# Layer 3's rows of the last image from x and z, with the product of two layers' weights, in a four-layer convolution and attention kernel

## The chip, the core and the metric

The kernel runs on one core of a Trainium2 chip. The metric is the device time of one execution in microseconds (us); lower is better. Before the change three executions took 2698.12 to 2698.23 us, median 2698.2.

## The reference, cut to what matters

Two images of 512 channels and 32 x 32 pixels go through four layers. Layers 0 and 1 (attention with offsets and a multilayer perceptron; attention by channel products with a batch normalization) aren't touched. Layer 2 is attention over the 1024 pixels with 128 middle channels; layer 3 is attention with one channel each for theta, phi and g, plus a squeeze-and-excitation weight.

```python
# layer 2
scores = jnp.einsum('bcn,bcm->bnm', f_x, g_x) * scale
attn = jax.nn.softmax(scores, axis=-1)
z = jnp.einsum('bnm,bcm->bcn', attn, h_x).reshape(B, mid, H, W)
z = conv1x1(z, wv, bv)
return z + x
# layer 3
x_avg = jnp.mean(x, axis=(2, 3), keepdims=True)
se_mid = jax.nn.relu(conv1x1(x_avg, se1_w, se1_b))
W_cw = jax.nn.sigmoid(conv1x1(se_mid, se2_w, se2_b))
g_x = conv1x1(x, g_w, g_b).reshape(b, N)
theta_x = conv1x1(x, theta_w, theta_b).reshape(b, N)
phi_x = conv1x1(x, phi_w, phi_b).reshape(b, N)
f_div_C = jax.nn.softmax(theta_x[:, :, None] * phi_x[:, None, :], axis=-1)
y = jnp.einsum('bij,bj->bi', f_div_C, g_x)
return W_cw * bn(conv1x1(y, W_w, W_b)) + x
```

Layer 3's rows theta, phi and g are linear in layer 2's output, which is x + wv z + bv. So w3 (x + wv z + bv) = w3 x + (w3 wv) z + w3 bv, and the rows can be had from layer 2's input x and from z, without layer 2's output.

## The kernel before, in words

Everything is float32, with channels on the 128 partitions, in four blocks of 128, and pixels along the free dimension, 1024 per image. Layers 0 and 1 take the first 2550 us or so. The last part of the program runs layers 2 and 3 for image 0, with layer 2 of image 1 woven in, and ends with the function `last` for image 1. `last` is written out by hand: each of its instructions goes through `pin`, which keeps it in program order on its engine. The rest is ordered by a scheduler. Each engine executes its own queue in order; semaphores stand where one engine needs another's result or a buffer that another still reads.

Image 0 ends in `l3_out`: `py`, the mean spread over all partitions, lies in two PSUM banks; VectorE reads it once (L1656), ScalarE scales the first result (L1657) and reads `py` three times (L1659), VectorE adds x to these three (L1660), and four stores go out on SP (L1661).

`last` then does this, in halves of 512 pixels:

- `out_z` (L1693): z, eight accumulating matmuls for each half, then a ScalarE copy to SBUF (L1694);
- `out_x` (L1699, L1702): for each half and block of channels one matmul of z with `l2wv`, and on VectorE the sum of that, the bias and x, written over x, with its pixel sum in `xavg`;
- `row` (L1711, L1716): the rows of layer 3, four matmuls for each half, one for each block of channels, each into 32 partitions of its own of `prow`, with weights `w3x`; then a ScalarE copy to `rows3` that adds the biases `b3` (L1672, L1674);
- `spread` (L1723) puts phi and g on all partitions (`pscore`), `turn` (L1728) transposes theta to the partitions (`ptl`), `theta` (L1732) adds up the four blocks' parts, `extremes` (L1735, L1736) finds the largest and smallest phi, and L1810 to L1812 make the exponents' offset of it;
- `exponential` (L1741, ScalarE, eight times) and `weighted` (L1754, VectorE, eight times): the softmax' numerator, denominator and weighted sum, with three buffers `e3` between them;
- the squeeze-and-excitation: `avg` (L1816, L1817), four matmuls (L1821), `mid` on ScalarE (L1826), four matmuls (L1828), `cw` and `aff` (L1831 to L1840);
- `raised` (L1776, GpSimd): the constant part added to x; `mean` (L1759, L1760, L1764): the weighted mean y, spread over all partitions (`pyl`);
- `final` (L1780, VectorE) or `final_act` (L1785 on ScalarE, then L1786 on GpSimd): the output, and its store (L1768, SP).

PSUM has eight banks. Four hold the two `pscore` tiles; two are a pool `ps` with two buffers, for `pz`, `pr2` and `pyl`; the last two are image 0's pool `gps` with one buffer of two banks (`py` is its last tile), and after it, in `last`, a pool `gpl` of two buffers of one bank each, for `prow`, `ptl` and `psel`:

```python
with tc.tile_pool(name="gps", bufs=1, space=PSUM) as gps:
    nd, part = l3_scores(0, gp, gps)
    ...
    l3_out(0, gp, gps, nd)
with tc.tile_pool(name="gpl", bufs=2, space=PSUM) as gps:
    last(1, fp, gp, fps, ps, gps, at2, ht)
```

Of the kernel before, what the change touches and what calls it, by code (L numbers as in the profile page):

```python
# [16 lines left out]
P = 128  # L17
# [3 lines left out]
KC = C // P  # L21
# [51 lines left out]
def conv_seq(  # L73
# [61 lines left out]
    with ExitStack() as ctx_l0:  # L135
# [51 lines left out]
        def pin(ins):  # L187
            return tc.keep_in_program_order(ins) if started else ins
# [890 lines left out]
    xsum = late.tile([P, KC, NT // 512], F32, name="xsum")  # L1079
    l2w = late.tile([P, KC, 3, MID], F32, name="l2w")  # L1080
    nc.sync.dma_start(l2w, l2_w)
    l2wv = late.tile([P, C], F32, name="l2wv")
    nc.sync.dma_start(l2wv, l2_wv)
    se1w = late.tile([P, KC, SE], F32, name="se1w")
    nc.sync.dma_start(se1w, se1_w)
# [576 lines left out]

    def last(b, fp, gp, fps, ps, gps, at2, ht):

        pin = tc.keep_in_program_order
        ve, pe, act = nc.vector, nc.tensor, nc.scalar

        b3 = gp.tile([P, 1], F32, name="b3")
        for i, name in enumerate(("theta", "phi", "g")):
# [4 lines left out]
                else ve.scalar_tensor_tensor(b3, ident[:, i : i + 1], v(f"L3_conv_{name}_b"), b3, ALU.mult, ALU.add)  # L1674
            )
        z = fp.tile([P, HW], F32, name="z")
        rows3 = gp.tile([P, 2, 512], F32, name="rows3")
        th = gp.tile([P, 8], F32, name="th")
        ext = gp.tile([P, 2, 2], F32, name="ext")
# [6 lines left out]
        def at(o, half):  # L1686
            return x[:, o, b * HW + half * 512 : b * HW + (half + 1) * 512]

        def out_z(half):
            pz = ps.tile([P, 512], F32, name="pz", tag="ps")  # L1690
            for t in range(8):
                rhs = at2[:, t, half * 512 : (half + 1) * 512]
                pin(pe.matmul(pz, lhsT=ht[:, t, :], rhs=rhs, start=(t == 0), stop=(t == 7)))  # L1693
            pin(act.copy(z[:, half * 512 : (half + 1) * 512], pz))  # L1694
# [9 lines left out]
                )  # L1704
            )

        def row(half, k):
            if k == 0:
                prow[half] = gps.tile([P, 512], F32, name=f"prow{half}", tag="l3")
            pin(  # L1710
                pe.matmul(  # L1711
                    prow[half][k * 32 : (k + 1) * 32, :], lhsT=w3x[:, k, :], rhs=at(k, half), start=True, stop=True
                )
            )
            if k == KC - 1:
                pin(act.activation(rows3[:, half, :], prow[half], AF.Identity, bias=b3))  # L1716


        pp = [fps.tile([P, 2, 512], F32, name="pscore") for _ in range(2)]
# [1 line left out]
        def spread(half, i):  # L1721
            to_all = c("sel3")[:, i : i + 1].to_broadcast([P, P])
            pin(pe.matmul(pp[i][:, half, :], lhsT=to_all, rhs=rows3[:, half, :], start=True, stop=True))  # L1723
# [63 lines left out]
            store(o, half, r)  # L1787

        es, py = {}, {}
        out_z(0)  # L1790
        out_z(1)
        for o in range(KC):
            out_x(0, o)
        for o in range(KC):
            out_x(1, o)
        for half in range(2):
            for k in range(KC):
                row(half, k)
        spread(0, 0)
        turn(0)  # L1800
        spread(1, 0)
        turn(1)
        extremes(0)
        theta(0)
        spread(0, 1)
        spread(1, 1)
        extremes(1)
        theta(1)
# [2 lines left out]
        pin(ve.tensor_scalar(nm[:, 1, :], th, top[:, 0:1], -1.0, ALU.mult, ALU.mult))  # L1811
        pin(ve.scalar_tensor_tensor(nm[:, 0, :], th, top[:, 1:2], nm[:, 1, :], ALU.mult, ALU.min))  # L1812
        exponential(0)

        avg = gp.tile([P, KC], F32, name="avg")
        pin(ve.tensor_tensor(avg, xavg[:, :, b, 0], xavg[:, :, b, 1], ALU.add))  # L1816
# [2 lines left out]
        for k in range(KC):  # L1819
            pin(  # L1820
                pe.matmul(  # L1821
                    pse[0:SE, 0, 0:1], lhsT=se1w[:, k, :], rhs=avg[:, k : k + 1], start=(k == 0), stop=(k == KC - 1)
                )
            )
        mid = gp.tile([SE, 1], F32, name="mid")
        pin(act.activation(mid, pse[0:SE, 0, 0:1], AF.Relu, bias=v("L3_conv_se1_b")[0:SE]))  # L1826
        for o in range(KC):
            pin(pe.matmul(pse[:, 1, o : o + 1], lhsT=se2w[:, o * P : (o + 1) * P], rhs=mid, start=True, stop=True))  # L1828
        weighted(0)
        cw = gp.tile([P, KC], F32, name="cw")  # L1830
        pin(ve.tensor_tensor(cw, pse[:, 1, 0:KC], v("L3_conv_se2_b"), ALU.add))  # L1831
        exponential(1)
        exponential(2)
        pin(act.activation(cw, cw, AF.Exp, scale=-1.0))
        weighted(1)
        weighted(2)
        pin(ve.tensor_scalar(cw, cw, 1.0, None, ALU.add))
        pin(ve.reciprocal(cw, cw))
        aff = gp.tile([P, 2, KC], F32, name="aff")
        pin(ve.tensor_tensor(aff, l3s, cw.unsqueeze(1).to_broadcast([P, 2, KC]), ALU.mult))  # L1840
        for half in range(2):
            for o in range(3 + half):
                raised(o, half)
        exponential(3)
        weighted(3)
        mean(0)
        for t in range(4, 8):
            exponential(t)
        weighted(4)
        weighted(5)  # L1850
        final(0, 0)
        final_act(3, 0)
        weighted(6)
        weighted(7)
        mean(1)
        final(1, 0)
        final(2, 0)
        for o in range(KC):
            final(o, 1)

    with tc.tile_pool(name="f", bufs=2) as fp, tc.tile_pool(name="g", bufs=1) as gp:
# [23 lines left out]
def _layout(a):  # L1885

    f = np.float32
    got = {k: np.asarray(x) for k, x in a.items()}

    def col(x):  # L1890
        return np.ascontiguousarray(x.reshape(-1, P).T)

    def kxn(x):

        return np.ascontiguousarray(x.T.reshape(-1, P, x.shape[0]).transpose(1, 0, 2))

    vecs = np.zeros((P, NV), f)
    for name, (at, w) in _AT.items():
        x = got[name]
        if name == "L0_conv_off_dw_w":  # L1900
            x = np.tile(x.reshape(DH, 36), (2, 1))
        elif name == "L0_conv_off_dw_b":
            x = np.tile(x, 2).reshape(P, 1)
        elif name == "L0_conv_cpb_w1":
            x = x.T
        elif name == "L3_conv_se1_b":
            vecs[:SE, at] = x
            continue
        elif x.size == 1:
            x = np.repeat(x.reshape(1, 1), P, 0)  # L1910
        else:
            x = col(x)
        vecs[:, at : at + w] = x
    rows = np.concatenate([got["L1_conv_bv"], got["L2_conv_bh"]])[None]

    consts = np.zeros((P, NCONST), f)

    order = np.zeros((P, NORDER), f)

    def put(name, x, to=consts):  # L1920
# [12 lines left out]
    put("npx", -(p % 32).astype(f)[:, None])  # L1933
    put("sel3", (p[:, None] % 32 == np.array([1, 2])[None]).astype(f))


    rank = p // 32 * 4 + p % 4
    same = p[:, None] % 32 // 4 == p[None] % 32 // 4
    put("same", same.astype(f), order)
    put("below", (same & (rank[:, None] < rank[None])).astype(f), order)  # L1940
    put("place", (np.array([0, 2, 1, 3])[p // 32] * 4 + p % 4).astype(f)[None], order)
    put("rank", rank.astype(f)[:, None], order)

    put("third", (np.arange(33)[None] == (1 + 8 * (p // 32) + 2 * (p % 4))[:, None]).astype(f), order)
    put("npy", -(4 * np.arange(8)[None] + p[:, None] // 32).astype(f))


    qkv = np.zeros((P, 3, KC, P), f)
    for i, name in enumerate(("qw", "kw", "vw")):
        w = got[f"L0_conv_{name}"].reshape(KC, 2, DH, DH)  # L1950
        for h in range(2):
            hs = slice(h * DH, (h + 1) * DH)
            qkv[hs, i, :, hs] = w[:, h].transpose(2, 0, 1)
    pw = got["L0_conv_off_pw_w"]
    off = np.zeros((P, P), f)
    for h in range(2):
        off[h * DH : (h + 1) * DH, h * 32 : (h + 1) * 32] = pw[0][:, None]
        off[h * DH : (h + 1) * DH, 64 + h :: 2] = pw[1][:, None]
    cpb = np.ascontiguousarray(got["L0_conv_cpb_w2"].T)

    return {
        "x": got["x"],
        "vecs": vecs,
        "rows": rows,
        "consts": consts,
        "order": order,
        "qkv_w": qkv,
        "off_w": off,
        "cpb_w": cpb,
        "out_w": kxn(got["L0_conv_out_w"]),  # L1970
        "mlp_w1": kxn(got["L0_conv_mlp_w1"]),
        "mlp_w2": kxn(got["L0_conv_mlp_w2"]),

        "l1_w": np.stack(
            [kxn(got["L1_conv_Wq"]), kxn(got["L1_conv_Wv"]), kxn(got["L1_conv_Wk"].T)]
            + [kxn(got["L1_conv_Wo"]), kxn(got["L1_conv_Wo"].T)],
            1,
        ),
        "l2_w": np.stack([kxn(got[f"L2_conv_{n}"]) for n in ("wf", "wg", "wh")], 2),
        "l2_wv": np.ascontiguousarray(got["L2_conv_wv"].T),  # L1980
        "se1_w": kxn(got["L3_conv_se1_w"]),
        "se2_w": np.ascontiguousarray(got["L3_conv_se2_w"].T),
    }
# [18 lines left out]
```

## Time and profile before

| What | us |
|---|---|
| profiled execution, its own time | 2697.67 |
| its span | 2695.9 |
| median of three runs | 2698.2 |
| TensorE / VectorE / ScalarE / GpSimd busy | 2653.6 / 2251.3 / 1538.4 / 669.8 |
| z of image 1, L1693, first start | 2644.28 |
| first `out_x` addition on VectorE, L1702 | 2659.08 |
| first exponential, L1741 | 2673.63 |
| last store issued, L1768 | 2692.2 |

The profile is of one execution; its times count from the start of the span. A float32 matmul is listed as two passes, so that x32 in a row stands for 16 matmuls. A chain of waits is followed back from the last instruction, each step to what released it. The windows list, for each stretch, the busy time of an engine and the clock that TensorE was granted (1.00 is full).

### The profile page before, as it was taken

How to read it: one execution, taken by the hardware profiler on the slowest of the kernel's cores; microseconds unless marked ns; L12 is line 12 of the kernel's file. 1: busy time of each engine (PE TensorE's matmuls, PEld its weight loads, DVE VectorE, ACT ScalarE, POOL GpSimd, SP SyncE). 2: the span in 40 equal slices, each digit the busy share in tenths (PEclk: the TensorE clock that was granted, in tenths of full speed). 3: DMA queues.
4: the chain of work that ended last, by engine and by line, in shares of the span. 5: the costliest groups of instructions: out<-in, count | busy, mean ns of one | idle time of the engine just before them, and what ended most of it. 6: DMA issues, size and time to landing. Idle time of an engine off the chain costs nothing.

```text
span 2695.9 us, 48423 instructions
## 1 busy us (share of the span) xinstructions
PE 2653.6 (98%) x19574; PEld 967.3 (36%) x19574; DVE 2251.3 (84%) x2009; ACT 1538.4 (57%) x1920; POOL 669.8 (25%) x784
## 2 busy tenths in 40 slices
PE   8999999999999999999999999999999999999997
PEld 4223323232332323333333333333444444455544
DVE  6999999999999999999999999999554445525646
ACT  7676677777667777866877776776221111001334
POOL 0333333333333333333333333333100000000001
PEclk9999999999999999999999999999999999999998
DMA  4777877877777787787788788787400000100001
GB/s 129 165 165 162 168 158 161 169 157 162 163 166 158 165 170 157 165 168 161 162 195 173 154 179 188 163 174 159 94 30 24 16 24 24 62 17 1 1 0 63
DMA packets 109327, 335.04 MB, mean 124 GB/s; under 512 B 18576, under 2 KB 28304, under 8 KB 108336
## 3 DMA queue, kind: packets, MB, share of 16 engines
q0 software_dynamic: 69632, 234.93, 46.7%
q1 hardware_dynamic: 38896, 96.51, 10.4%
q8 instruction: 154, 2.52, 0.4%
q14 instruction: 69, 0.57, 0.1%
q10 hardware_dynamic: 576, 0.51, 0.1%
HBM read 58.99 MB, written 4.46 MB: 24 GB/s over the span
## 4 chain that ended last, share of the span: by engine, by line
PE 81%; DVE 9%; issue 6%; ACT 2%; DMA 1%; POOL 1%; DVEq 0%; ACTq 0%; POOLq 0%
PE ph L619 51%; DVE h L353 4%; PE A L1105 4%; PE D L1105 4%; PE C L1105 4%; DVE r L634 3%; PE B L1105 2%; PE po L1040 2%; PE pg L1248 1%; PE pa L1359 1%; PE pu L1282 1%; PE psim L664 1%; PE pscore L1491 1%; DMA xs<-r 1%; PE pt L1511 1%
## 5 line engine op out<-in xcount | busy, mean ns | idle before, releaser
L619 PE MATMUL ph<-h,w2a 128*32 128x512 f32 x16384 | 1779.1, 593 | 6.0 <-ACT r L628 3.3
L628 ACT ACTIVATE r<-ph,sb 128x1024 f32<-128x1024 f32 x1024 | 1141.1, 1114 | 510.5 <-PE ph L619 487.3
L353 DVE CUSTOM_DVE_ANT_1 h<-tab 128x2048 f32<-128x2048 f32 x512 | 1172.9, 2291 | 13.0 <-PE ph L619 10.0
L619 PEld LDWEIGHTS ph<-h,w2a 128*32 128x32 f32 x16384 | 520.2, 109 | 1226.6 <-issue 801.7
L634 DVE SCALAR_TENSOR_TENSOR r<-r,rel,r 128x1024 f32<-128x1024 f32 x512 | 658.0, 1285 | 16.4 <-ACT r L628 15.8
L642 POOL DMA_DIRECT2D r<-r x256 | 219.5, 857 | 961.2 <-DMA r<-r 936.1
L637 POOL DMA_DIRECT2D r<-r x256 | 245.2, 958 | 280.4 <-DVE r L634 243.6
L653 POOL DMA_DIRECT2D xs<-r x256 | 306.6, 1198 | 12.2 <-issue 6.1
L173 ACT ACTIVATE tab<-tab,vec 128x256 f32<-128x256 f32 x252 | 136.9, 543 | 0.0
L1293 POOL MEMSET M<- 128x512 f32 x2 | 1.0, 524 | 435.3 <-DVE x L1169 435.3
L1145 ACT COPY u<-A 128x512 f32<-128x512 f32 x16 | 9.4, 585 | 146.9 <-PE A L1105 146.9
L1776 POOL TENSOR_TENSOR x<-x,aff 128x512 f32<-128x512 f32 x7 | 7.0, 1031 | 329.0 <-ACT e L1741 329.0
L1124 ACT ACTIVATE h<-h,vec 128x512 f32<-128x512 f32 x32 | 23.1, 721 | 113.7 <-DVE h L1127 113.7
L1127 DVE TENSOR_TENSOR h<-C,u 128x512 f32<-128x512 f32 x32 | 22.1, 691 | 48.2 <-PE C L1105 47.9
L1105 PE MATMUL A<-xn,w 128*128 128x512 f32 x128 | 60.3, 593 | 0.8 <-DVE x L1047 0.8
L1105 PE MATMUL C<-hT,w 128*128 128x512 f32 x128 | 60.3, 592 | 0.0
L1105 PE MATMUL A<-h,w 128*128 128x512 f32 x128 | 60.1, 592 | 0.0
L1040 PE MATMUL po<-q,vwo 128*128 128x512 f32 x128 | 56.3, 594 | 0.0
L230 DVE SCALAR_TENSOR_TENSOR acc<-q,vec,acc 128x128 f32<-128x128 f32 (+3 forms) x88 | 46.2, 525 | 0.8
L1165 DVE TENSOR_TENSOR x<-D,x 128x512 f32<-128x512 f32 x32 | 22.1, 691 | 25.8 <-PE D L1105 25.7
L856 ACT ACTIVATE e<-e,den 128x64 f32<-128x64 f32 x128 | 41.8, 338 | 1.9 <-DVE den L852 1.9
L1165 DVE TENSOR_TENSOR x<-C,x 128x512 f32<-128x512 f32 x32 | 22.1, 690 | 24.8 <-PE C L1105 24.8
(365 smaller groups left out, 1867.6 us busy)
## 6 DMA issues: line engine op xcount, KB each, us to landing
r<-r POOLq DMA_DIRECT2D x256, 512.0 KB, 5.2
r<-r POOLq DMA_DIRECT2D x256, 256.0 KB, 3.4
xs<-r SPq DMA_DIRECT2D x256, 128.0 KB, 3.9
xs<-r POOLq DMA_DIRECT2D x256, 128.0 KB, 5.6
tab<-fd SPq DMA_DIRECT2D x63, 512.0 KB, 5.6
lw<-in_l_w_dram SPq DMA_DIRECT2D x5, 1024.0 KB, 9.0
x<-in_x_dram SPq DMA_DIRECT2D x4, 1024.0 KB, 10.5
w<-in_mlp_w_dram SPq DMA_DIRECT2D x8, 512.0 KB, 4.3
```

Source lines behind the costliest of these rows:

```text
L173: return nc.scalar.activation(tf, tf if src is None else src[:, :, ax, :], AF.Identity, bias=0.0 if ax == 0 else v("L0_conv_cpb_b1"), scal ...
L230: pin(nc.vector.scalar_tensor_tensor(dst, src, wt_, dst, ALU.mult, ALU.add))
L353: nc.vector._custom_dve(TENSOR_ADD_SAT, out=h1, in0=columns.unsqueeze(1).to_broadcast([P, 32, 2, 32]), in1=rows_.unsqueeze(3).to_broadcast ...
L619: nc.tensor.matmul(ph[t * 32 : (t + 1) * 32, i, :], lhsT=w2a[:, o], rhs=h1s[2 * p + i][:, half * 16 : (half + 1) * 16, h, :], start=True, ...
L628: pin(nc.scalar.activation(r, ph, AF.Relu, bias=sb3[:, o, 1:2]))
L634: pin(nc.vector.scalar_tensor_tensor(r0, r1, rel[:, i : i + 1], r0, ALU.mult, ALU.add))
L637: pin(nc.gpsimd.dma_start(rs[p, 0], rs.pop((p, 2)), accum_op=ALU.add))
L642: pin(nc.gpsimd.dma_start(r[0::2], r[1::2], accum_op=ALU.add))
L653: pin(nc.gpsimd.dma_start(xs_[t][d::4], rs.pop((p, 0))[2::4], accum_op=ALU.add))
L1040: nc.tensor.matmul(po, lhsT=vwo[:, k * B + t // 2, o * P : (o + 1) * P], rhs=q[:, k, ts_], start=(k == 0), stop=(k == KC - 1),)
L1105: nc.tensor.matmul(banks[bank], lhsT=a[an][k], rhs=b_[bn_][k], start=(i < 4 and k == 0), stop=(k == n - 1), skip_group_check=True,)
L1165: nc.vector.tensor_tensor(to, t, to, ALU.add)
```

## The change

The weights `l2_wv` are loaded twice as wide: transposed as before, and once more as they are, in blocks. Ahead of z, `weights_z` multiplies them with `w3x` into `w3z` (128 x 32) and adds the product of `w3x` and layer 2's bias to `b3`. The row matmuls then run on x before it is overwritten (`rows_x`), leaving their sums open in PSUM, and on z as soon as a half of it is there (`rows_z`), each block of 32 partitions taking a quarter of the half's pixels. Only the first half's first two outputs of `out_x` stay ahead of the exponentials; the other six stand between them. The squeeze-and-excitation and the finals are moved accordingly: five `raised` instead of seven, three `final_act` instead of one.

```diff
-    l2wv = late.tile([P, C], F32, name="l2wv")
+    l2wv = late.tile([P, 2 * C], F32, name="l2wv")
...
+        w3z = gp.tile([P, 32], F32, name="w3z")
...
-        def out_z(half):
+        def out_z(half, between={}):
             pz = ps.tile([P, 512], F32, name="pz", tag="ps")
             for t in range(8):
+                for fn, *args in between.get(t, ()):
+                    fn(*args)
...
-        def row(half, k):
...
+        def weights_z():
+            pw = gps.tile([P, 33], F32, name="pwz", tag="l3")
+            for k in range(KC):
+                wk = l2wv[:, C + k * MID : C + (k + 1) * MID]
+                pin(pe.matmul(pw[:, 0:32], lhsT=wk, rhs=w3x[:, k, :], start=(k == 0), stop=(k == KC - 1)))
+            for k in range(KC):
+                pin(
+                    pe.matmul(
+                        pw[0:32, 32:33],
+                        lhsT=w3x[:, k, :],
+                        rhs=v("L2_conv_bv", k),
+                        start=False,
+                        stop=(k == KC - 1),
+                        skip_group_check=True,
+                    )
+                )
+            pin(ve.tensor_copy(w3z, pw[:, 0:32]))
+            pin(ve.tensor_tensor(b3[0:32], b3[0:32], pw[0:32, 32:33], ALU.add))
+
+        def rows_x(half):
+            prow[half] = gps.tile([P, 512], F32, name=f"prow{half}", tag="l3")
+            for k in range(KC):
...
+                        prow[half][k * 32 : (k + 1) * 32, :],
+                        lhsT=w3x[:, k, :],
+                        rhs=at(k, half),
+                        start=True,
+                        stop=False,
...
+        def rows_z(half):
+            for k in range(KC):
+                ks = slice(k * P, (k + 1) * P)
...
+                        prow[half][k * 32 : (k + 1) * 32, ks],
+                        lhsT=w3z,
+                        rhs=z[:, half * 512 + k * P : half * 512 + (k + 1) * P],
+                        start=False,
+                        stop=True,
...
+            pin(act.activation(rows3[:, half, :], prow[half], AF.Identity, bias=b3))
...
+        weights_z()
+        rows_x(0)
+        rows_x(1)
         out_z(0)
-        out_z(1)
-        for o in range(KC):
-            out_x(0, o)
-        for o in range(KC):
-            out_x(1, o)
-        for half in range(2):
-            for k in range(KC):
-                row(half, k)
-        spread(0, 0)
-        turn(0)
+        out_z(1, {2: [(rows_z, 0)], 5: [(spread, 0, 0), (turn, 0), (spread, 0, 1)]})
+        extremes(0)
+        theta(0)
+        out_x(0, 0)
+        rows_z(1)
+        out_x(0, 1)
         spread(1, 0)
         turn(1)
-        extremes(0)
-        theta(0)
-        spread(0, 1)
         spread(1, 1)
         extremes(1)
         theta(1)
...
         exponential(0)
+        out_x(0, 2)
+        out_x(0, 3)
+        weighted(0)
+        exponential(1)
+        exponential(2)
+        out_x(1, 0)
+        out_x(1, 1)
+        weighted(1)
+        out_x(1, 2)
+        out_x(1, 3)
...
+        exponential(3)
         mid = gp.tile([SE, 1], F32, name="mid")
...
-        weighted(0)
+        weighted(2)
         cw = gp.tile([P, KC], F32, name="cw")
         pin(ve.tensor_tensor(cw, pse[:, 1, 0:KC], v("L3_conv_se2_b"), ALU.add))
-        exponential(1)
-        exponential(2)
         pin(act.activation(cw, cw, AF.Exp, scale=-1.0))
-        weighted(1)
-        weighted(2)
+        exponential(4)
+        weighted(3)
...
-        for half in range(2):
-            for o in range(3 + half):
-                raised(o, half)
-        exponential(3)
-        weighted(3)
+        for half, o in ((0, 0), (0, 1), (1, 0), (1, 1), (1, 2)):
+            raised(o, half)
         mean(0)
-        for t in range(4, 8):
+        for t in range(5, 8):
             exponential(t)
         weighted(4)
         weighted(5)
-        final(0, 0)
+        final_act(2, 0)
         final_act(3, 0)
         weighted(6)
         weighted(7)
         mean(1)
+        final(0, 0)
         final(1, 0)
-        final(2, 0)
-        for o in range(KC):
+        final_act(3, 1)
+        for o in range(KC - 1):
             final(o, 1)
```

More of the change, by code (lines that the diff above doesn't have):

```diff
@@ L1705, in out_x @@
             )
-        def row(half, k):
[L1708 to L1712, printed above, removed]
-                )
-            )
-            if k == KC - 1:
-                pin(act.activation(rows3[:, half, :], prow[half], AF.Identity, bias=b3))
+        def weights_z():
[13 more added lines that the diff above has]
+                    )
+                )
+            pin(ve.tensor_copy(w3z, pw[:, 0:32]))
+            pin(ve.tensor_tensor(b3[0:32], b3[0:32], pw[0:32, 32:33], ALU.add))
@@ new lines, in rows_x @@
+        def rows_x(half):
+            prow[half] = gps.tile([P, 512], F32, name=f"prow{half}", tag="l3")
+            for k in range(KC):
+                pin(
+                    pe.matmul(
+                        prow[half][k * 32 : (k + 1) * 32, :],
[3 more added lines that the diff above has]
+                        stop=False,
+                        skip_group_check=True,
+                    )
+                )
@@ new lines, in rows_z @@
+        def rows_z(half):
+            for k in range(KC):
+                ks = slice(k * P, (k + 1) * P)
+                pin(
+                    pe.matmul(
+                        prow[half][k * 32 : (k + 1) * 32, ks],
[3 more added lines that the diff above has]
+                        stop=True,
+                        skip_group_check=True,
+                    )
+                )
+            pin(act.activation(rows3[:, half, :], prow[half], AF.Identity, bias=b3))
@@ L1979, in _layout @@
         "l2_w": np.stack([kxn(got[f"L2_conv_{n}"]) for n in ("wf", "wg", "wh")], 2),
-        "l2_wv": np.ascontiguousarray(got["L2_conv_wv"].T),
+        "l2_wv": np.concatenate(
+            [got["L2_conv_wv"].T, got["L2_conv_wv"].reshape(KC, P, MID).transpose(1, 0, 2).reshape(P, -1)], axis=1
+        ),
         "se1_w": kxn(got["L3_conv_se1_w"]),
```

## The prediction

> **What bounds the kernel now.** I read the page first (TensorE busy for 98% of the span), then the chain of waits over the last 55 us, then the timeline and the windows of the same stretch, since everything that the diff touches runs there. The chain, in order of time (start, us, what):
> ```profile
> 2643.33 1.12 PE py L1645 x10
> 2644.45 13.73 PE pz L1693 x32
> 2658.18 7.73 PE pr L1699 x16
> 2665.92 1.90 PE prow L1711 x16
> ...
> 2673.36 0.24 DVE nm L1812
> 2673.60 0.02 issue
> 2673.63 1.29 ACT e L1741 x2
> ...
> 2691.50 0.66 DVE rl L1780
> ```
> TensorE carries the end until 2667.8: z (16 matmuls of 0.86 us), eight layer-2 outputs (0.97 us each, paced by VectorE and two buffers), the rows. Then VectorE carries it. I call the start of the first exponential E; it is at 2673.63, so 22.27 us of the 2695.9 follow. Any gain must make E earlier by more than what it puts behind E.
>
> The timeline at the border between the images (start, us, engine, line, operation, shapes, count, idle before):
> ```profile
> 2646.86 3.38 ACT L1659 ACTIVATE r<-py,aff 128x1024 f32<-128x1024 f32 x3
> ...
> 2648.08 3.50 DVE L1660 TENSOR_TENSOR r<-r,x 128x1024 f32<-128x1024 f32 x3 [2.31 <-ACT r L1659]
> ...
> 2651.68 0.47 DVE L1674 SCALAR_TENSOR_TENSOR b<-cst,vec,b 128x1 f32<-128x1 f32 x2
> ```
> While TensorE computes z, ScalarE still reads image 0's `py` from PSUM until 2646.86 + 3.38 = 2650.24, and VectorE is busy with image 0 and `b3` until 2652.15. Today nobody on TensorE waits for them.
>
> TensorE's clock after a short pause (stretch, length, PE busy, clock, DMA share, GB/s), and one late wait:
> ```profile
> 2672.50:2673.00 0.50, 0.00 (x0) 1.00 0.00 0
> ...
> 2674.50:2675.00 0.50, 0.00 (x0) 1.00 0.00 0
> 2675.00:2675.50 0.50, 0.39 (x3) 0.83 0.00 0
> 2675.50:2676.00 0.50, 0.50 (x4) 0.50 0.00 0
> ...
> 2689.43 2.73 DVE L1780 SCALAR_TENSOR_TENSOR rl<-pyl,aff,x 128x512 f32<-128x512 f32 x4 [0.92 <-PE pyl L1764]
> ```
> The dense matmuls stop at 2672.42 and 2.9 us later the clock is halved, although 0.39 us of small matmuls lay between.
>
> **What the Trainium skill says.** "PSUM — Partial Sum Buffer", section "PSUM bank collisions raise a hardware error": engines must be kept apart by bank, reads against reads too. The trace agrees: the one ScalarE final (L1785) waited 0.57 us for VectorE's final on the same `pyl`. "TensorE: Matmul & The Clock Gate", Part 1: the clock halves after about 3.4 us of idleness and comes back after a busy window of about 3.4 us, the windows running freely. The trace shows the fall (above); no run so far shows the return. Same page, Part 3: matmuls start and end in program order. The chain agrees: no matmul there overtakes another.
>
> **The change part by part.** Durations are from the profiled execution (2697.67 us, 1.77 outside its span). The median of the runs is 2698.2; I add the difference to that.
>
> 1. *A hold before z.* `weights_z` is now the first work of the last image on TensorE, ahead of z. Its tile `pwz` comes from the two-bank pool that takes over the banks of image 0's `py`. The built program says so: the first `pwz` matmul waits for the VectorE read (L1656 of before) and for the third ScalarE read (L1659) of `py`. Before, the first user of these banks was `prow`, 21 us later, and found them free. So TensorE stands still from 2644.45 to 2650.27: **+5.8**. Behind it are queued all 16 z matmuls, and every later step waits for z.
>
> 2. *New TensorE work before z.* Four 128x32 products with 128-column weights: nearest row L1631, 1.05 us for four such weight loads. Four bias products with 32-column weights: L1821, 0.39. The eight row matmuls, moved here from after the outputs: 1.90. Sum 3.34, so z starts at 2653.6 at full clock. `prow1` also waits for VectorE's `w3z` copy and `b3` add, as it reuses `pwz`'s bank; VectorE is free at 2652.15, two small operations (0.17 each, as L1637) end at 2652.5, when `prow0` is just finishing at 2652.66. So that wait costs nothing.
>
> 3. *The clock.* A 5.8 us pause is twice the 2.9 us that sufficed above. At half rate these steps take 1.69 (measured for L1828) + 0.78 + 3.8 = 6.3 us. Bounds: nothing lost, if the clock stays up; or half rate until 2657, about 3.2 lost. Estimate from the page's window: back at full rate near 2655.3, by when 5.0 us at half rate have done 2.5; the rest is 0.6 to 0.8. z starts at 2655.9: **+2.3**.
>
> 4. *From z to E.* z's first half 6.87; two matmuls of the second 1.72; `rows_z` 0.3 (eight passes side by side in four column groups as in `prow`; between 0.25 and 0.9, the ends being full overlap and none); three z matmuls 2.57, hiding the 0.69 of `rows3`; spread, turn, spread 0.86 + 0.44 + 0.86; three z matmuls 2.57; an output 0.86 (hiding the z copy of 0.58), `rows_z` 0.3, an output 0.86 (hiding `rows3`), spread 0.88. Then as before, two extremes, theta, top and two scalings: 2673.63 - 2671.59 = 2.04. Sum 21.2; before, z start to E took 29.18. So **-8.0**, less the 3.34 of part 2. E is at 2655.9 + 21.2 = 2677.1, that is **+3.5**.
>
> 5. *After E.* Before, VectorE issued its last final so that the last store went out at 2692.19, E + 18.56. Now six of the eight output additions (0.69 each on the chain of such operations) lie behind E. In us after E: additions of two outputs end at 1.7 (TensorE makes the second at 0.95); `weighted(0)` 2.9 (1.15 each); two additions 4.25; `weighted(1)` 5.4; two additions 6.8; averages 7.1; `weighted(2)` 8.25. Here VectorE waits for the squeeze chain, matmul 0.45, ScalarE 0.28, matmul 1.73 at half clock: 9.6, a wait of 1.35 (0.73 before). `cw` and `weighted(3)` 10.9; the sigmoid's end and `aff` 11.5; mean 11.85; four `weighted` 16.45; mean 17.0 (0.1 and up to 0.53, as L1759 and L1760). `pyl1` takes 2.09 at half clock: 19.1. Now `final_act(3,1)` reads `pyl1` first, and the program's waits make VectorE's last three finals follow it: 19.9, then 3 x 0.67 = 21.9. GpSimd adds `final_act(3,1)` at 21.1, and its store stands ahead of three others on SP; at SP's pitch of 0.43 (2688.42 to 2688.85) the last goes out near 22.5. Four stores then overlap more closely than before (0.66 apart); I add 0.1 for it, between 0 and 0.5. ScalarE's eight exponentials are done by 14.8 and the three finals on ScalarE and GpSimd take two finals, 1.35, off VectorE; without that cover it would be 23.9. Tail: 22.6 + 3.71 (2692.19 to 2695.9) = 26.3 against 22.27: **+4.0**.
>
> 6. *At nothing:* the double width of the `l2wv` load, issued at 1962.77 and first read at 2582; if it were late it would cost at most its 0.7 us of transfer (a 256 KB store's pitch). The scheduler leaves the order before the tail as it was. SP holds eight output stores as before, in another order; GpSimd seven operations of 1.0 each becoming eight, five of them raising x.
>
> Sum: +5.8 + 3.34 + 2.3 - 8.0 + 4.0 = **+7.5** (rounded), so 2698.2 + 7.5 = **2705.7**, 0.28% slower. No change means within 0.2%, 5.4 us, 2692.8 to 2703.6.
>
> **The rivals.**
> - *The clock stays up.* The hold is there, but TensorE resumes at full rate: +5.2, 2703.4, not slower by the bound. For it: the windows run freely and the trace shows only one fall in the middle of light work. Against: twice the pause, empty. It decides if less than half of the 2.3 is lost. 20%.
> - *No hold.* The waits are met when `pwz` comes, and the change does what it says: z at 2647.8, E at 2669.0, -4.6 + 4.0: 2697.6. It needs `py` to be read by 2644.45, and ScalarE's reads begin only at 2646.86. 6%.
> - *The tail costs little.* VectorE's additions fall into waits that it has anyway (1.08, 0.73 and 0.92 before): the tail's +4.0 becomes about 0, 2701.7. Against: those waits come at other places, and two return longer. 7%.
> - *The clock stays at half through z's first half:* another 6 us, 2712. For it: from 2675.5 on the clock never came back in this trace; against: nothing dense ran there. 7%.
>
> **How the numbers follow.** Forecast 60%, rivals 20, 6, 7, 7. The forecast's own range is 2703.5 to 2708: the clock from 0.5 to 3.2, the tail's stores and means about 1. The range reaches down to 2701.5 for the first and third rival, up to 2708.5; left out are no hold and half clock through z, and the edges. Slower: 0.57 + 0.08 + 0.07 = 0.72. Faster only if no hold meets a short tail: 0.02. Same: 0.26.
>
> **What would show it.** Right: a TensorE gap of about 5.8 us before `pwz`, ended by ScalarE's L1660 (L1659 before); a clock of 0.5 after it; E near 2677; VectorE's last three finals behind a ScalarE final; the last store near E + 22.5. Wrong: z starting before 2650 (part 1 falls), full clock at 2651 to 2655 (part 3), E to the end under 25 us (part 5).

## The result, and the profile after

The changed kernel takes 2707.05 us, the median of six executions (2706.54 to 2707.14), against 2698.03 for the kernel before on the same chip (six executions, 2696.46 to 2698.23). The ratio is 1.0035, with a 95% interval from 1.0023 to 1.0047: slower by more than the 0.2% that can be told from no change. The profiled execution took 2706.54, with a span of 2704.8.

The chain that ended last, of the changed kernel, from the border between the images (start, us, what):
```profile
2643.71 1.13 PE py L1646 x10
2644.84 0.03 issue
2644.87 1.29 DVE r L1657
...
2647.24 3.39 ACT r L1660 x3
2650.62 0.04 issue
2650.67 1.92 PE pwz L1719 x8
2652.58 0.46 PE pwz L1723 x7
2653.05 2.98 PE prow L1739 x14
2656.03 8.78 PE pz L1701 x20
...
2689.80 5.02 POOL x L1824 x5
2694.82 2.46 POOL rl L1834 x2
2697.28 0.02 issue
2697.30 2.05 DMA out_dram<-rl
...
2699.44 0.75 DVE rl L1828
```
In the kernel before, `pz` followed `py` at once. Here the chain leaves TensorE for VectorE and ScalarE, which still read image 0's `py`, and comes back 5.83 us later with `pwz`. z starts at 2656.03. The end of the chain is new as well. VectorE's last final still ends it, but it no longer waits for the mean. The finals have six buffers `rl` for eight outputs, so the last one waits until the second store has landed, and that store waited for GpSimd.

The timeline of the changed kernel at the places that the prediction named (start, us, engine, line, operation, shapes, count, idle before):
```profile
2650.67 1.92 PE L1719 MATMUL pwz<-w3x,l2wv 128*128 128x32 f32 x8 [5.84 <-ACT r L1660]
...
2677.90 1.21 ACT L1789 ACTIVATE e<-pscore,nm,th 128x1024 f32<-128x1024 f32 x1 [3.26 <-DVE nm L1856]
...
2687.70 0.16 DVE L1886 TENSOR_TENSOR cw<-psel,vec 128x4 f32<-128x4 f32 x1 [1.56 <-PE psel L1883]
...
2697.89 2.29 DVE L1828 SCALAR_TENSOR_TENSOR rl<-pyl,aff,x 128x512 f32<-128x512 f32 x3 [1.73 <-ACT rl L1833]
```
So E, the start of the first exponential, is 2677.90, and 26.9 us follow it. (In the changed kernel L1789 is an exponential, L1886 `cw`, L1824 `raised`, L1828 VectorE's `final`, and L1833 and L1834 are `final_act` on ScalarE and GpSimd.)

Windows of the changed kernel (stretch, length, PE busy, clock, DMA share, GB/s):
```profile
2648.50:2649.00 0.50, 0.00 (x0) 0.53 1.01 410
...
2655.00:2655.50 0.50, 0.50 (x8) 0.64 0.06 25
```
Of the first, 0.06 of the half microsecond is at full clock ((0.53 - 0.5) / 0.5), so the clock fell at 2648.53. Of the second, 0.28 is, so it came back at 2655.36. All of `pwz` and most of `prow` ran at half rate.

The start of the border, S (the end of image 0's `py`), lies between 2643.35 and 2645.67 in the profiled executions of this study, and repeated executions of one kernel spread over up to 3.5 us. The clock has a part in this. The kernel before has a pause of 2.74 us on TensorE near 2564, after which the clock is at half rate from 2566.11 to 2569.52:
```profile
2566.00:2566.50 0.50, 0.00 (x0) 0.61 0.00 0
...
2569.50:2570.00 0.50, 0.50 (x3) 0.98 0.00 0
```
Nine of the twelve profiled executions show such a fall, and in them S is 2644.45 or later; the other three (e2, e5 and e8) don't, and in them it is 2643.35 to 2643.91. So the parts after S are compared from S on, each from one profiled execution. Where kernels share a stretch they agree closely: S to E is the same within 0.02 us in e1, e4, e5 and e6.

| profiled execution | S | S to E | E to end | S to end |
|---|---|---|---|---|
| before | 2644.45 | 29.18 | 22.27 | 51.45 |
| after | 2644.84 | 33.06 | 26.90 | 59.96 |

The change costs 8.5 us behind S: 3.9 ahead of E and 4.6 behind it. The other 0.39 between the two profiles is S itself.

### The profile page after: what moved, and what is told of

Read it like the earlier page. It is cut to its first block, busy times and chain, and to the rows that moved or that the text cites. A ratio compares the mean times of both kernels' runs of the same rounds, so it can differ in the third digit from the quotient of the medians.

```text
span 2704.8 us, 48489 instructions
## 1 busy us (share of the span) xinstructions
PE 2658.1 (98%) x19606; PEld 970.4 (36%) x19606; DVE 2249.8 (83%) x2009; ACT 1540.8 (57%) x1922; POOL 670.5 (25%) x784
## 4 chain that ended last, share of the span: by engine, by line
PE 82%; DVE 8%; issue 5%; ACT 2%; POOL 1%; DMA 1%; DVEq 0%; ACTq 0%; POOLq 0%
PE ph L619 52%; PE A L1106 4%; PE D L1106 4%; PE C L1106 4%; DVE h L353 3%; DVE r L634 2%; PE B L1106 2%; PE po L1040 2%; PE pg L1249 1%; PE pa L1360 1%; PE pu L1283 1%; PE psim L664 1%; PE pscore L1492 1%; DMA xs<-r 1%; PE pz L1521 1%
## 5 line engine op out<-in xcount | busy, mean ns | idle before, releaser
L1824 POOL TENSOR_TENSOR x<-x,aff 128x512 f32<-128x512 f32 x5 | 5.0, 1031 | 338.5 <-DVE y L1808 338.5
```

## The experiments

### One: is it the hold?

Three kernels, which part the hold from the clock and from the rest. The first (e1) takes the hold out of the changed kernel: the weights' product and the rows of x come after z's first half, when ScalarE has read `py`.
```diff
-        weights_z()
-        rows_x(0)
-        rows_x(1)
         out_z(0)
+        weights_z()
+        rows_x(0)
+        rows_x(1)
```


> The changed kernel with the products of the weights and the row matmuls on x moved behind z's first half on TensorE; nothing else. Hold theory (the first pwz matmul waits for ScalarE's last read of py, and the clock falls meanwhile): z starts near 2644.5, no TensorE gap over 1 us before the exponentials, clock 1.00 throughout, the first exponential 5.8 + 2.4 = 8.2 us earlier than in the changed kernel (near 2669.7), about 2699 in all, 8 us less than the changed kernel. Rival (the time goes to the tail or to the added matmuls, and the hold is hidden): at most 2 us less than the changed kernel's 2707.

Measured: 2697.43 us (2695.99 to 2698.71), before 2697.75 on that chip, ratio 0.9999 (0.999 to 1.0007). Its chain of waits:
```profile
2645.13 6.87 PE pz L1701 x16
2652.00 0.81 PE pwz L1719 x8
2652.81 0.31 PE pwz L1723 x7
2653.12 1.78 PE prow L1739 x14
2654.89 1.91 PE pz L1701 x4
```
TensorE goes from `py` to z without a pause, and `pwz`, which took 1.92 in the changed kernel, takes 0.81. From S, E comes at 24.76 (8.3 sooner than in the changed kernel, for the 8.2 expected) and the end at 50.97: 9.0 under the changed kernel, and only 0.5 under the kernel before.

The second (e2) keeps the hold and fills it: six z matmuls into a bank that nobody reads go ahead of the weights' product in the changed kernel.
```diff
+        pf = ps.tile([P, 512], F32, name="pfill", tag="ps")
+        for t in range(6):
+            pin(pe.matmul(pf, lhsT=ht[:, t, :], rhs=at2[:, t, 0:512], start=(t == 0), stop=(t == 5)))
         weights_z()
```


> The changed kernel with six z matmuls (5.15 us) ahead of the products, into a bank that nobody reads, so that TensorE is busy while it would wait; the wait for py itself stays. If the clock is worth what the forecast said: pwz still starts 5.8 us after image 0's last matmul, but at full clock, z starts 2.3 to 2.5 us earlier than in the changed kernel, about 2704.6. Rival (half clock costs nothing, because the added work is bound by weight loads or semaphores): z starts as in the changed kernel, 2707.

Measured: 2703.54 us (2702.06 to 2704.09), ratio 1.0021 (1.0013 to 1.0029). Its chain of waits:
```profile
2645.88 3.38 ACT r L1660 x3
2649.26 0.04 issue
2649.31 1.08 PE pwz L1719 x8
2650.39 0.31 PE pwz L1723 x7
2650.70 1.78 PE prow L1739 x14
2652.47 8.78 PE pz L1701 x20
```
The hold is there (S is 2643.48, `pwz` starts 5.83 later), but from `pwz` to z it takes 3.16 and not 5.36. So the clock costs 2.20 ahead of z, a little under the 2.3 to 2.5 expected. The squeeze's second matmuls also take 1.06 for 1.72, which the changed kernel lost to a second fall of the clock. S to end is 57.02: 2.9 under the changed kernel.

The third (e3) puts the hold alone into the kernel before: one small unread matmul into the first buffer of the pool that takes over `py`'s banks.
```diff
+        first = gps.tile([P, 512], F32, name="first", tag="l3")
+        pin(pe.matmul(first[0:32, 0:128], lhsT=w3x[:, 0, :], rhs=at(0, 0)[:, 0:128], start=True, stop=True))
         out_z(0)
```


> The kernel before with one small matmul (128 columns, its result not read) ahead of z, into the first buffer of the pool that takes over py's banks; rows, order and tail as before. Hold theory: z starts 5.8 us later and at half clock until the next full window has passed, which costs z 2.3 to 3.3 us more; about 8.5 us over before, 2706.5. Rival (image 0's reads would not hold a matmul, or the later stage has slack for it): within 1 us of before.

Measured: 2705.87 us (2704.75 to 2706.97), ratio 1.0031 (1.0019 to 1.0042). Chain of waits of this run, then its windows:
```profile
2647.42 3.29 ACT r L1659 x3
2650.71 0.04 issue
2650.76 0.63 PE first L1791 x2
2651.39 16.75 PE pz L1693 x32
```
```profile
2650.00:2650.50 0.50, 0.00 (x0) 0.69 0.00 0
...
2657.00:2657.50 0.50, 0.50 (x2) 0.98 0.00 0
```
z takes 16.75 for the 13.73 of before, 3.02 more. The clock is at half rate from 2650.19 to 2657.02, which covers 5.6 us of z, so some 2.8 of it is the clock's; the other 0.2 is what matmuls after a 32-column one took more in other runs too (part 4 below). With 5.84 of pause and 0.63 for the small matmul this makes E 9.5 later from S (38.66 for 29.18). The hold alone costs about what the whole change costs.

What follows: the prediction's parts 1 and 3 are shown. Taking the hold out gives back the 9.0, putting it alone into the kernel before costs as much, and filling it with work separates the clock's 2.20. And the changed kernel without its hold only equals the kernel before. Its gain ahead of E (4.4) is given back behind E (3.9).

### Two: what sets the end behind E?

All of these start from the kernel without the hold. The first (e4) takes VectorE's wait for the squeeze away by giving it a product to do, and moves the exponentials and the first mean to suit.
```diff
         exponential(3)
+        exponential(4)
         mid = gp.tile([SE, 1], F32, name="mid")
...
         weighted(2)
+        weighted(3)
+        exponential(5)
         cw = gp.tile([P, KC], F32, name="cw")
...
         pin(act.activation(cw, cw, AF.Exp, scale=-1.0))
-        exponential(4)
-        weighted(3)
+        mean(0)
```


> Base is the run with weights and rows behind z's first half (e1). In it VectorE's product 3 is brought ahead of the squeeze's result, ScalarE's exponentials 4 and 5 ahead of it, and the mean of the first half ahead of the sigmoid's end, so that VectorE's wait for the squeeze matmul (0.90 in e1, 1.56 in the changed kernel) has work in its place. Theory 1 (VectorE's chain alone sets the end, as the prediction's sum after E has it): the wait goes, VectorE's last product and the last store come 0.9 earlier, end 0.9 under e1. Theory 2 (the stores set the end: in e1 SP's second store waits for GpSimd's second addition, and from 2689.3 on the DMA engines move 380 GB/s without a pause until 2694.2): VectorE's last product comes 0.9 earlier, but GpSimd's additions and the first stores stay where they were, and the end moves by 0.3 or less.

Measured: 2696.96 us (2695.21 to 2697.61), ratio 0.9998 (0.999 to 1.0006). S to end is 50.30, 0.67 less, between the two theories. The chain of waits shows why:
```profile
2680.58 5.02 POOL x L1824 x5
2685.60 2.46 POOL rl L1834 x2
2688.06 0.02 issue
2688.07 2.05 DMA out_dram<-rl
...
2690.22 0.75 DVE rl L1828
```
The end hangs on GpSimd: five rows raised once `aff` is known, two additions, then the second store, for whose buffer VectorE's last final waits. With the wait gone, `aff` came 0.64 earlier (GpSimd starts at E + 10.61 for E + 11.25), and the end moved by that. So theory 2 names the chain, but I had overlooked that the edit brings `aff` forward too.

The second (e5) changes the finals: VectorE's write into x in place, the last ScalarE final becomes VectorE's, and GpSimd's additions come between the rows that it raises.
```diff
-            r = gp.tile([P, 512], F32, name="rl", bufs=6)
+            r = at(o, half)
             pin(ve.scalar_tensor_tensor(r, py[half], aff[:, 0, o : o + 1], at(o, half), ALU.mult, ALU.add))
...
+        final_act(2, 0)
         final(0, 0)
+        final_act(3, 0)
+        raised(1, 1)
+        raised(2, 1)
+        raised(3, 1)
```


> Base is e1. VectorE's finals write into x in place (no buffer to wait for), the last final of layer 3 is VectorE's and not ScalarE's, GpSimd makes its two additions ahead of the last three rows that it raises, and the stores stand on SP in the order in which they become ready. VectorE's products and its wait for the squeeze stay. Theory 1 (VectorE's chain alone sets the end): only the step on ScalarE (0.78 for 0.67) goes, end 0.2 under e1. Theory 2 (the stores): the eight stores start about 1 earlier and without the pause before the third, end 0.5 to 1.0 under e1.

Measured: 2696.47 us (2695.94 to 2698.56), ratio 1.0 (0.9992 to 1.0008), and from S 51.05: no gain. ScalarE's timeline has the reason:
```profile
2685.14 0.78 ACT L1833 ACTIVATE rl<-pyl,aff 128x512 f32<-128x512 f32 x1 [2.06 <-DVE x L1828]
```
With VectorE's final between ScalarE's two, on the same bank, ScalarE waited 2.06, GpSimd stood still for 1.57 behind it, and the rows raised last came late for VectorE's finals. A miss: neither theory had this. These waits hide what the rest of the change to the finals is worth.

The third (e6) joins the two edits and adds five unread z matmuls around the first half's mean, to keep TensorE's clock up; the fourth (e7) also makes the weights' product during image 0's layer 2, in the bank of its h tiles, and takes it out of the stretch behind S.
```diff
+        for t in range(1):
+            pin(pe.matmul(warm, lhsT=ht[:, t, :], rhs=at2[:, t, 0:512], start=(t == 0), stop=False))
+        mean(0)
+        for t in range(4):
+            pin(pe.matmul(warm, lhsT=ht[:, t, :], rhs=at2[:, t, 512:1024], start=False, stop=(t == 3)))
```
```diff
                 l2_out(0, fp, ps, at2, ht)
+                w3z, bz = weights_z(gp, psh)
...
         out_z(0)
-        weights_z()
```

> Base is e1, with both of the above, and five unread z matmuls (0.86 each at full clock) around the first half's mean, so that TensorE's clock is still full when the last mean needs it: pyl1 takes 1.05 and not 2.08. If the tail is made of both chains (VectorE's and the stores'): VectorE's last final ends near E + 20 (E + 21.6 in e1), the end is 2.0 to 2.5 under e1. If the stores alone set it: 1.0 under e1 at most. If the clock falls in spite of the five matmuls, they run at 1.7 each and the last mean comes 2 later than in e1: slower by 1 to 2.

> As e6, with the product of the weights made during the first image's layer 2 (in the bank of its h tiles), not behind z's first half. It takes 1.12 of TensorE out of the stretch between z's start and E; whether its matmuls cost as much where they go depends on whether TensorE waits there for others. Expected 0.5 to 1.1 under e6, and so some 2.5 to 3.5 under before (0.9988). If the first image's layer 2 has no room on TensorE: equal to e6.

Measured: 2696.54 us (2694.84 to 2697.15), ratio 0.9997 (0.9989 to 1.0005), and 2696.40 (2694.41 to 2697.37), the same ratio and interval. From S the ends are 49.87 and 48.84. The last mean did find the full clock (its `pyl` takes 1.05 and 1.16, for 2.08). In e7 the clock stayed up until then; in e6 it fell in spite of the five matmuls and was back in time, as its windows show:
```profile
2679.50:2680.00 0.50, 0.50 (x4) 0.87 0.00 0
...
2683.00:2683.50 0.50, 0.50 (x2) 0.72 0.00 0
```
That is half rate from 2679.87 to 2683.28. But GpSimd stood still for 1.85 ahead of its second addition, as in the run above, and the gain of e6 is 1.1 rather than 2.0 or more. The early product saves 1.05 between S and E (23.72 for 24.77), at the upper end of what I expected, but it isn't free where it now runs. From image 0's scores near 2562 to S, e7 takes 83.03 and e6 82.67, both with the clock's fall near 2567; e8 takes 81.58 and e5 81.00, both without it. So 0.4 to 0.6 of the 1.05 is lost ahead of S, and the medians of e6 and e7 differ by only 0.14.

The fifth (e8) undoes that pause: ScalarE makes both finals first, and GpSimd raises four rows, adds twice, and raises two. The sixth (e10) puts an unread matmul into TensorE's pause ahead of the squeeze, and orders the first stores as they become ready. The expectation speaks of moving one of the five; the kernel has all five where they were, and one more ahead of the squeeze.
```diff
-        raised(0, 0)
-        raised(1, 0)
-        raised(0, 1)
+        for o, half in ((0, 0), (1, 0), (0, 1), (1, 1)):
+            raised(o, half)
...
         final_act(2, 0)
-        final(0, 0)
         final_act(3, 0)
-        raised(1, 1)
         raised(2, 1)
         raised(3, 1)
+        final(0, 0)
```
```diff
+        pin(pe.matmul(warm, lhsT=ht[:, 0, :], rhs=at2[:, 0, 0:512], start=True, stop=False))
         pse = gps.tile([P, 2, 256], F32, name="psel", tag="l3")
...
+        pin(pe.matmul(warm, lhsT=ht[:, 1, :], rhs=at2[:, 1, 0:512], start=False, stop=False))
         mean(0)
...
+        store(2, 0, r2)
         final(0, 0)
+        store(3, 0, r3)
         final(1, 0)
```


> As e7, but ScalarE makes both its finals of the first half before VectorE's, and GpSimd raises four rows, adds twice, and raises the last two. In e5, e6 and e7 ScalarE's second final waited for VectorE's final on the same bank and GpSimd stood still for 1.6 to 1.9 before its second addition, so that VectorE's last three finals waited for rows raised behind it. If that is what sets the end there, VectorE's last final ends near E + 19.9 (E + 21.8 in e7) and the end is 1.1 under e7, where the eight stores at 380 GB/s then bind: some 2 to 2.5 under before (0.9992). If it doesn't: equal to e7.

> As e8, with one of the unread z matmuls moved ahead of the squeeze, into TensorE's pause of 1.6 after the last output, and the first half's stores in the order in which they become ready. In e8 the clock had fallen in that pause: the squeeze's second matmuls took 1.86 for 1.05, the unread ones 2.08 for 1.13, and the last mean began 0.9 after its operand. If the pause is what let the clock fall, the squeeze takes 1.05 and the last mean starts with its operand: VectorE's last final ends near E + 20.2 (E + 21.35 in e8), and as the stores then bind (eight at 380 GB/s), the end is some 0.5 under e8: about 2.5 under before (0.9991). If the fall has another cause: equal to e8.

Measured: 2695.75 us (2693.72 to 2697.06), ratio 0.9995 (0.9986 to 1.0003), and 2695.29 (2693.34 to 2696.86), ratio 0.9992 (0.9984 to 1.0000). In the fifth GpSimd no longer pauses, but the clock fell at 2675.52, in a stretch with little on TensorE; the unread matmuls then ran at half rate, the last mean started 0.9 after its operand, and from S nothing was gained (48.99), where 1.1 under e7 was expected. In the sixth the clock stayed up until the means were done. Its VectorE timeline, then its DMA view from 2684 to 2700 (GB/s in 40 slices of 0.4 us):
```profile
2685.20 4.12 DVE L1828 SCALAR_TENSOR_TENSOR x<-pyl,aff,x 128x512 f32<-128x512 f32 x6
```
```profile
GB/s 0 0 0 0 0 271 364 369 384 379 379 399 369 389 389 359 399 379 374 41 0 0 0 0 0 0 0 0 0 0 0 0 0 0 0 0 0 0 0 0
```
VectorE's six finals run without a gap and end at E + 19.9, and the eight stores of 256 KB, 2.1 MB, pass in one piece at about 380 GB/s. S to end is 47.73, 1.26 under e8 and 3.7 under the kernel before; counted from 2562, so that the early product is in it, 2.9 under the kernel before.

That the added matmul kept the clock up is not shown. Up to the squeeze e7 has the same work and the same pause without it, and its clock stayed up too, until 2686.88. Its windows at the end of that pause and at the fall:
```profile
2676.50:2677.00 0.50, 0.37 (x8) 1.00 0.00 0
...
2686.50:2687.00 0.50, 0.00 (x0) 0.88 0.58 213
```
So e7 and e8 differ in whether the clock fell in a stretch that they share. Of the two, e7 is the fairer base for e10: both had the full clock, and e10 ends 1.1 sooner from S, as much as GpSimd's new order was expected to give (the stores' new order is in it too). Part of e8's miss, and of the step from e8 to e10, is where the pause happened to fall.

The sixth is the best version here. By the median it is 2.2 us under the kernel before, and its interval ends at no change, so it is a small gain that these executions do not quite secure.

The last one (e9) asks where the tail's loss comes from: it is the kernel without the hold, with all eight outputs of layer 2 and their additions ahead of E.
```diff
+        out_x(0, 2)
+        out_x(0, 3)
+        for o in range(KC):
+            out_x(1, o)
         extremes(1)
         theta(1)
```


> Base is e1, with all eight of layer 2's outputs and additions ahead of the second half's extremes, so ahead of E; nothing else. Theory 1 (the prediction's: E's gain and the tail's loss are largely the same six additions in another place): E comes about 7 later (six outputs at TensorE's 0.86 stand in front, and the scalings after them), the time from E to the end falls by 4.1 for the additions and 0.9 for the squeeze's wait, from 26.2 to about 21.2; the end is some 2 above e1. Theory 2 (the tail is long because of the finals' new split over three engines and of the stores, not because of the additions): E comes 7 later, the time from E stays at 25 or more, the end is 6 above e1.

Measured: 2702.25 us (2701.42 to 2703.46), ratio 1.0019 (1.0012 to 1.0027). E comes 7.7 later from S (32.42 for 24.76), and E to the end is 24.05, between the theories. Its VectorE timeline:
```profile
2678.37 1.22 DVE L1802 SCALAR_TENSOR_TENSOR e<-e,pscore 128x1024 f32<-128x1024 f32 x1 [1.08 <-ACT e L1789]
...
2684.05 0.16 DVE L1884 TENSOR_TENSOR cw<-psel,vec 128x4 f32<-128x4 f32 x1 [2.07 <-PE psel L1881]
```
The six additions are gone from behind E, but I had left the squeeze queued on ScalarE behind the fourth exponential. So VectorE now waits 1.08 for the first exponential and 2.07 for the squeeze, whose second matmuls met half clock as well (1.88 for 1.06). `aff` ends 8.8 behind E, for 10.9 in the kernel without the hold, and the end follows it by about as much. This speaks for theory 1, but it isn't a clean test: the additions' own 4.1 did not appear in full, as waits took part of their place.

## Why the prediction was right

The forecast was 2705.7 and the median 2707.05, so 1.35 short. The mechanism held: a hold, a fallen clock, a shorter way to E and a longer one behind it. In the profiles the shortfall is part 4 (0.7), part 5 (0.6) and S (0.4), against parts 2 and 3, which together took 0.3 less than forecast.

**Part 1, the hold (+5.8).** Right: 5.83, by the engine and line named. The run with the hold alone shows that it needs nothing else of the change.

**Part 2, the new work ahead of z (+3.34).** With the clock up it takes 3.16, in the run with the filled hold. That `prow1`'s own wait costs nothing also held: TensorE goes through the rows there without a pause.

**Part 3, the clock (+2.3).** 2.20, by the filled hold. The clock came back at 2655.36 for the 2655.3 of the estimate, and z started at 2656.03 for 2655.9 (though S was 0.39 later). This was closer than the argument deserved, and in part luck: the same hold in the kernel before cost some 2.8 of clock, since the fall and the return came later there. The prediction also says that no run so far shows the clock's return. The kernel before does, ahead of the stretch that was read: half rate from 2566.11 to 2569.52, after a pause of only 2.74 us. That pair of windows stands above; it would have shown that the clock comes back within a few microseconds of dense work.

**Part 4, z to E (21.2).** 21.87. Three terms were small by 0.2 each: the groups of matmuls that follow the 32-column `prow` took 1.91 for 1.72, 2.77 for 2.57 and 1.06 for 0.86. The kernel without the hold shows the same three numbers within 0.01, also at full clock; the cause is open. The two `rows_z` took 0.36 for 0.3. E is at 2677.90 for 2677.1.

**Part 5, behind E (+4.0).** +4.6, but the end is not reached as I had it. VectorE did go as predicted up to the last product (E + 16.35 for 16.45), and its last three finals wait for ScalarE's. But the path that ends last leaves VectorE at `aff` (E + 11.6 for 11.5), goes through GpSimd's five raised rows (5.02) and two additions (2.46), and then through seven stores. SP's second store waits for the second addition, at 2697.28, and everything behind it on SP waits too. The DMA view of the changed kernel, 2694 to 2704 in slices of 0.25 us:
```profile
GB/s 0 0 0 0 0 0 0 0 0 0 0 123 393 377 156 0 172 377 385 369 401 361 385 377 377 377 393 385 401 385 353 410 361 385 369 320 0 0 0 0
```
From the pause on the engines move some 380 GB/s without a break: 0.69 us for each 256 KB. From the end of GpSimd's second addition to the end of the span it takes 7.5 us here and in the kernels that keep these seven stores behind it (e1, e2, e4, e8 and e9). VectorE's last final waits on the same second store, for its buffer, and ends at E + 22.3 for 21.9; but its own store then takes 2.86 to land, for 2.05 of the second, as it queues behind the others.

The kernel before ends in the same way, which the prediction doesn't have. There GpSimd's one addition ends at 2688.40 and releases SP's second store; this and the six behind it land 0.63 to 0.72 apart, and the end is 7.5 later. Its DMA view, 2686 to 2696 in slices of 0.25 us:
```profile
GB/s 0 0 0 0 0 0 0 0 0 0 0 0 0 344 369 393 377 401 377 377 401 369 401 352 352 401 377 385 401 377 393 393 99 0 0 0 0 0 0 0
```
So the +4.6 is how much later after E the addition ends that releases the second store: E + 19.4 for E + 14.8. `aff` came 5.4 later, GpSimd raised two rows fewer (2.0) and made one addition more (1.2).

The sum came near because its own path is nearly as long. It put the last store's issue at E + 22.5, and that is at E + 22.7. The mis-sized term is "I add 0.1 for it, between 0 and 0.5": from the last issue to the end it was 4.2, for 3.7 before, so 0.5. GpSimd's second addition and the order of the stores on SP were in the sum's text, but not in its path.

**Part 6, at nothing.** Of GpSimd the prediction says that seven operations of 1.0 each become eight. There were eight before too, seven raised rows of 1.0 and one addition of 1.25; now five rows and three additions. The count was wrong, and GpSimd is on the path. S came 0.39 later than before in the profiled execution. As S moves by up to 2.3 us between the profiles, this neither shows nor rules out a cost of the double load.

**The rivals.** "No hold" gave 2697.6 for a kernel whose waits are met; the kernel without the hold measured 2697.43. So the sum also holds with the hold taken out: -4.4 ahead of E and +3.9 behind it, for the -4.6 and +4.0 of that rival. "The clock stays up" gave 2703.4; the filled hold measured 2703.54. "The tail costs little" fell by the 26.9 behind E, and "half clock through z's first half" by the return at 2655.36.

## What to carry to other kernels

In this kernel the first user of a pool of banks that takes over from another waited 5.83 us for the last reader of the old tile, and everything behind it on TensorE waited too. Look for such a border, and put work that needs no new bank first: the move of three calls behind z's first half was worth 9 us. Work that is moved from ahead of a milestone to behind it is only a gain if something else has time for it there: the kernel without the hold has E 4.4 us earlier from S and ends within 0.1% of the kernel before. At an end made of stores, count the store that is released late, the stores queued behind it and the buffers that they free, not only the last arithmetic.

Before a step between two profiles is put down to an edit, look whether the clock fell in a stretch that both share, as between e7 and e8. And time counted from a milestone leaves out what an edit moved ahead of it, as with the early product.

## What the runs showed of the hardware

**The clock keeps a grid.** In the changed kernel TensorE's clock was at half rate from 2648.53 to 2655.36, in the kernel before with the hold from 2650.19 to 2657.02: 6.83 us in both, though TensorE resumed at 2650.67 and at 2650.76. In the run e8, without any hold, it was so again. Its windows:
```profile
2675.50:2676.00 0.50, 0.40 (x2) 0.52 0.00 0
...
2682.00:2682.50 0.50, 0.50 (x2) 0.65 0.00 0
```
That is 2675.52 to 2682.35, 6.83 once more. In e6 (2679.87 to 2683.28) and in the kernel before (2566.11 to 2569.52) half rate lasted 3.41, half of that. In the changed kernel the next fall, at 2686.08 (0.58 in the window from 2686.00), comes 30.72 after the return, nine times 3.41. This agrees with the Trainium skill, "TensorE: Matmul & The Clock Gate", Part 1, which has activity counted in free-running windows of about 3.4 us. In these traces the same pause costs more or less by where it meets the grid: the hold 2.20 in the changed kernel and some 2.8 in the kernel before, and the pause near 2564 nothing in e5 and a stretch of half clock in the kernel before.

The page speaks of an idle window. In e8 the window that ended at 2675.52 wasn't empty: outputs ran in it until 2673.2 and four of the squeeze's small matmuls (0.39) after them, 1.48 us of listed TensorE time in all, and the clock fell. In e7 a window with 1.75, which holds the same pause (2673.22 to 2676.64, counted back from the fall at 2686.88), was followed by full clock. In e6 the fall followed a window with 2.38, of which 1.44 are the squeeze's matmuls of one column. So the listed busy time alone doesn't tell when the clock falls, and where the border lies is open.

**Unread matmuls as a filler.** Six of them in the hold kept the clock up and saved 2.20 us. In the tail the last mean's matmuls took between 1.05 and 1.16 for 2.08 with five or six of them, though in e6 the clock fell and came back meanwhile. Where the clock had fallen ahead of them, in e8, they stood in the way for 0.9.
